# Two reorderings in a convolution, softmax and whitening kernel: when a bias is given out, and when one interpolation is

## Chip, cores and metric

The kernel runs on one core of one Trainium2 chip. The time is the device time of one execution in microseconds, and the median of several runs is given. An engine is named as the profile names it: PE is TensorE, DVE is VectorE, ACT is ScalarE, POOL is GpSimd, SP is SyncE, which here issues most DMAs.

## What is computed

The input x has 4 images of 256 channels and 64x64 pixels, in float32. The first layer is a local attention: a 7x7 convolution with dilation 2 to 128 channels, a 1x1 convolution to 49 channels, a softmax over the 49, and a sum of the 49 shifted copies of x, weighted with the softmax. The second layer whitens the result over groups of 64 channels.

```python
k = lax.conv_general_dilated(x, w1, (1, 1), [(6, 6), (6, 6)], rhs_dilation=(2, 2), ...) + b1
k = lax.conv_general_dilated(k, w2, (1, 1), ...) + b2
attn = jax.nn.softmax(k, axis=1)
shifts = stack([xp[:, :, 2*u:2*u+64, 2*v:2*v+64] for u in range(7) for v in range(7)], axis=1)
x = jnp.einsum('bkchw,bkhw->bchw', shifts, attn)
...
Sigma = EPS * I + einsum('gdm,gem->gde', xc, xc) / m      # groups of 64 channels
for _ in range(5): P = 1.5 * P - 0.5 * (P @ P @ P) @ Sigma_N
X_hat = (P * sqrt(rTr)) @ xc * weight + bias
```

## The kernel before

**The convolution.** The two convolutions have no nonlinearity between them, so the kernel multiplies their weights once and does one 7x7 convolution from 256 to 49 channels. It does it by evaluation and interpolation, in rows and in columns (a Toom-Cook scheme): image rows are combined into 7 row points, each of them is combined along the columns into 7 column points, each point needs a short convolution (six of the row points this way, the seventh directly, line 685), and the outputs are interpolated back, first along the columns and then along the rows. One row point, br, passes through these steps:

- `weights` (line 364) gets the weights of the point. For most points they are loaded from DRAM by a DMA on SP (line 378, `wr<-gd`), which may start once the matmuls of the row point before have left the buffer.
- `row_eval` (line 439) makes the row combination `rb` on DVE, and `col_ops` (line 473) the column points `xh` on DVE, with one copy on ACT (lines 488 and 494). Each `xh` has one buffer, which PE must have left before the next row point is written.
- `conv_bank` (line 520) does the matmuls of a bank of column points into PSUM (lines 538 to 546) and evicts them to `pv` with an ACT copy (line 548). There are three banks a row point, with 3, 3 and 1 column points. Images 1 to 3 use two slots of `pv` in turn, so that row 2 writes over row 0.
- `col_interp` (line 617) interpolates the columns with 20 DVE instructions into `zz`, and a last ACT copy, `end` (line 635).
- After the fifth and the sixth row point, `row_interp` (line 643) interpolates the rows in two parts into `lgx`, the logits. It writes four phases. Each phase gets the convolution's bias in an ACT instruction (line 662).

**The order.** `conv_step(k, i)` (line 738) is given out for each row point k and bank i: the bank's matmuls, then `prepare`, which evaluates bank i for the row point after, and after the last bank the interpolation. The instructions that are given out are then put in order on each engine's queue when the program is built: the planner takes, by its own estimate of when things are ready, the ready instruction that was given out first, except that instructions inside `tc.high_priority()` count as earlier. On the chip each queue then runs in that fixed order.

Two things are put off by hand. The ACT instructions behind an interpolation (`end`) are put on a list `later` and are given out behind the eviction of the second bank of the next row point (lines 552 to 562), each with a dependency that holds it behind that eviction. This holds for the copy of `col_interp` and for the two biases of the first part of `row_interp`, for images 1 to 3. The list is emptied from its end.

**The work beside it.** While the convolution of image b runs, the output of an earlier image is made in eight phases an image, from a plan: `gap(b, j)` (line 1247) gives out `first_half(n)` or `second_half(n)` at eight points between the conv steps. Such a half transposes blocks of x on PE (line 1032) and copies them out of PSUM on ACT (line 1040, `xb`), multiplies them with a banded matrix of the softmax weights (line 1061, `y<-band,xb`), moves the result on ACT (line 1080), transposes it (line 1093), copies it (line 1101, `yt<-tp`, high priority) and adds to the second moments (line 1114). The transposes share three PSUM tiles `tp`. The band is loaded by DMAs on SP (line 994, `band<-sd`) and then transposed in place on DVE (line 1009). `softmax` of an image is in two halves; for image 0 the second half stands in the plan between the conv steps of image 1's rows 0 and 1.

Of the kernel before, what the change touches and what calls it, by code (L numbers as in the profile page):

```python
# [32 lines left out]
def kernel(  # L33
# [55 lines left out]
    def taps(b):  # L89
        return (0,) if b == INF else (0, 1)  # L90

    def pe(ins):
        return tc.keep_in_program_order(ins)
# [203 lines left out]
    @contextmanager  # L297
    def in_order():
        was = strict[0]
        strict[0] = True  # L300
        with tc.high_priority():
            yield
        strict[0] = was
# [198 lines left out]
    def col_eval(src, i):  # L502
        for _ in col_ops(src, i):
            pass
# [10 lines left out]

    slot = {}

    later = []

    def conv_bank(b, br, i, w):  # L520

        if i == 0:
            slot[b, br] = len(slot) % NV if b == 0 else (len(slot) - NV) % 2
        pts = BANKS[i]
        i0 = sum(len(k) for k in BANKS[:i])
        cv = cv_buf[ncv[0] % 2][:, : 3 * PT].rearrange(
            "p (n q b two) -> p n q b two", n=3, two=2, b=Q9
        )
        ncv[0] += 1
        for k, bc in enumerate(pts):  # L530
            terms = [(sr, sc, cc) for sc in taps(bc) for sr in taps(br) for cc in range(NCC)]
            wv = w[bc].rearrange("p c (a r k) -> p c r a k", r=len(taps(br)), a=NCC)
            for j, (sr, sc, cc) in enumerate(terms):

                n = Q9 if j == 0 and bc == INF else Q8
                for h in range(2):
                    pe(
                        nc.tensor.matmul(  # L538
                            cv[h * HB : h * HB + KT, k, sr : sr + n, sc : sc + n],
                            wv[:, sc, sr, cc],  # L540
                            xh[bc][:, :n, h * NCC + cc, :n],
                            start=(j == 0),
                            stop=(j == len(terms) - 1),
                            skip_group_check=True,
                        )
                    )
        with tc.high_priority():
            last = nc.scalar.copy(  # L548
                pv[:K2, slot[b, br], i0 : i0 + len(pts)].rearrange("p n q b -> p (n q b)"),
                cv[:K2, : len(pts)].rearrange("p n q b two -> p (n q b two)"),  # L550
            )
        if i == 1:

            while later:
                tc.add_manual_dep(
                    later.pop()().ins,
                    last.ins.name,
                    mybir.DependencyInfo(
                        mybir.DependencyClass.NoSync, mybir.DependencyReason.DATA
                    ),  # L560
                    reason="later",
                )

    def interpolate(pt, tmp, outs, cut, part=None, pairs=None):

        lo = lambda t: cut(t, 0)
        hi = lambda t: cut(t, 1)
        c0, s1, s2, s3, s4, hh, c6 = (pt[b] for b in (0, 1, 2, 3, 4, 5, 6))
        both = tmp
        if pairs is not None:
            tmp, s1 = tmp[:, 0], tmp[:, 1]
        if part != 1:
            if pairs is not None:  # L580
                add(both, *pairs)
                sub(pairs[1], *pairs)
            else:
                add(tmp, s1, s2)
                sub(s2, s1, s2)
                add(s1, s3, s4)
                sub(s4, s3, s4)
            add(s3, c0, c6)
            madd(s1, tmp, -2.0, s1)
            sub(s3, tmp, s3)  # L590
            madd(tmp, tmp, -30.5, s1)
            sub(s4, s4, s2)
            madd(tmp, s3, 22.5, tmp)
            madd(s1, c0, 1.5, s1)
            madd(tmp, s2, -16.0, tmp)
            madd(s1, c6, -30.0, s1)
            if part is None:
                add(tmp, tmp, s4)
            madd(s3, s1, -1.0 / 6, s3)
            madd(outs[0], lo(s1), 1.0 / 6, hi(c0))  # L600
            if part == 0:
                add(outs[2], lo(c6), hi(s3))
                add(s3, tmp, s4)
        if part != 0:
            madd(hh, tmp if part is None else s3, -1.0 / 9, hh)
            if part is None:
                add(outs[2], lo(c6), hi(s3))
            madd(s4, hh, -3.0, s4)
            sub(s2, s2, hh)
            madd(s2, s4, -1.0 / 15, s2)  # L610
            madd(outs[1], lo(s4), 1.0 / 15, hi(s2))

    def phases(t):

        return [t[..., bass.ds(4 + a - R if a < R else 0, Q8, 4), :] for a in range(4)]

    def col_interp(b, br, part=None):
        at = slot[b, br]
        pt = {
            c: pv[:K2, at, i].rearrange("p q b -> p (q b)").rearrange(  # L620
                "p (q b two) -> p q b two", q=Q9, two=2
            )
            for i, c in enumerate(ORDER)
        }
        outs = phases(zz[:K2, br].rearrange("p q (w two) -> p q w two", two=2))
        cut = lambda t, k: t[:, :, k : k + Q8]
        t = ct.rearrange("p a b -> p (a b)") if b == 0 else spare[:, NTAP:]
        t = t[:K2, : 2 * PT].rearrange("p (n q b two) -> p n q b two", q=Q9, two=2, n=2)
        pair = lambda i: pv[:K2, at, i : i + 4 : 3].rearrange(
            "p n q b -> p n (q b)"  # L630
        ).rearrange("p n (q b two) -> p n q b two", q=Q9, two=2)
        interpolate(pt, t, outs, cut, part, (pair(0), pair(1)))

        def end():
            ins = nc.scalar.copy(outs[3], cut(pt[5], 0))
            return ins

        if part is None and b > 0 and br != ROWS[-2]:
            later.append(end)
        elif part != 0:  # L640
            end()

    def row_interp(b, part):

        pt = {k: zz[:K2, k] for k in range(NP)}
        lg = lgx
        if b == 0:
            lg = store[4].rearrange("p c r w -> p (c r w)")
        lg = lg[:, : SH * W].rearrange("p (r w) -> p r w", w=W)
        outs = phases(lg[:K2])  # L650
        cut = lambda t, k: t[:, k : k + Q8]
        tr = ct.rearrange("p a b -> p (a b)")[:K2, : Q9 * W].rearrange("p (q w) -> p q w", w=W)
        interpolate(pt, tr, outs, cut, part)
        if part == 0:
            done_ = ((0, outs[0]), (2, outs[2]))
        else:
            done_ = ((3, cut(pt[5], 0)), (1, outs[1]))
            logits[b] = lg
        for a, t in done_:

            def end(a=a, t=t):
                return nc.scalar.activation(outs[a], t, AF.Identity, bias=bias[:K2])

            if b > 0 and part == 0:
                later.append(end)
            else:
                end()

# [55 lines left out]
    rows = [(0, br) for br in (1, 2, 3)]  # L724
    NR0 = len(rows)
    rows += [(b, br) for b in range(1, B) for br in ROWS]
    cur, nxt = {}, {}

    def prepare(k, i):

        b, br = rows[k]
        w = weights(b, br, i)
        if i == 0:
            cur["x"] = row_eval(b, br)
        nxt.update(w)
        col_eval(cur["x"], i)

    def conv_step(k, i):
        w = {bc: nxt.pop(bc) for bc in BANKS[i]}
        b, br = rows[k]  # L740
        conv_bank(b, br, i, w)
        end = b > 0 and br == ROWS[-1]
        if end:

            with in_order():
                if i == len(BANKS) - 2:
                    col_interp(b, br, 0)
                elif i == len(BANKS) - 1:
                    col_interp(b, br, 1)
                    row_interp(b, 1)  # L750
        if k + 1 < len(rows):
            prepare(k + 1, i)
        if i == len(BANKS) - 1 and not end:
            last = br == ROWS[-2]
            with in_order() if last else nullcontext():
                col_interp(b, br)
                if last:
                    row_interp(b, 0)
# [17 lines left out]
    def bank(k, i):  # L776
        conv_bank(0, rows[k][1], i, {bc: nxt.pop(bc) for bc in BANKS[i]})
# [60 lines left out]
    direct0(5, 0)  # L838
    col_interp(0, 3)
    row_interp(0, 0)  # L840
    prepare(NR0, 0)
    direct0(5, 1)
# [646 lines left out]
```

## Time and profile before

| | |
|---|---|
| Runs | 747.56 us median (745.64, 747.56, 749.41) |
| The profiled execution | 746.19 us, of which the span of the trace is 744.4 us |
| PE matmul busy | 703.4 us, 94% of the span |
| DVE busy | 611.3 us, 82% |
| ACT busy | 332.5 us, 45% |
| Mean granted PE clock | 0.986 |
| Image 1's convolution on PE, row 0's first matmul to row 5's last | 156.9 to 278.2 us |

In the profile a row of a timeline gives the start and the length in us, the engine, the line, the operation, its output and inputs, and in brackets how long the engine was idle before and what ended that. A table of stages gives for each stretch of time its length, the busy time of PE, PE's weight loads, DVE, ACT and POOL with the number of instructions, then the granted PE clock, the DMA engines' busy share and the GB/s moved.

### The profile page before, as it was taken

How to read it: one execution, taken by the hardware profiler on the slowest of the kernel's cores; microseconds unless marked ns; L12 is line 12 of the kernel's file. 1: busy time of each engine (PE TensorE's matmuls, PEld its weight loads, DVE VectorE, ACT ScalarE, POOL GpSimd, SP SyncE). 2: the span in 40 equal slices, each digit the busy share in tenths (PEclk: the TensorE clock that was granted, in tenths of full speed). 3: DMA queues.
4: the chain of work that ended last, by engine and by line, in shares of the span. 5: the costliest groups of instructions: out<-in, count | busy, mean ns of one | idle time of the engine just before them, and what ended most of it. 6: DMA issues, size and time to landing. Idle time of an engine off the chain costs nothing.

```text
span 744.4 us, 18491 instructions
## 1 busy us (share of the span) xinstructions
PE 703.4 (94%) x7512; PEld 528.3 (71%) x7512; DVE 611.3 (82%) x1268; ACT 332.5 (45%) x953; POOL 51.6 (7%) x52
## 2 busy tenths in 40 slices
PE   6999999997999897999999999999999889998996
PEld 1449543377898794799998958898998678885331
DVE  3789998999999989968995999799969655535575
ACT  1424240255364543466444435735535663322564
POOL 0410070020001110001000100000000000000000
PEclk9999999999899999999999999999999999999999
DMA  8991120147263491076545820534423144371588
GB/s 319 250 319 73 60 88 12 60 147 212 87 193 112 146 317 48 21 245 199 185 128 201 253 69 7 166 108 135 155 64 95 32 149 118 104 296 72 219 357 327
DMA packets 59629, 114.41 MB, mean 154 GB/s; under 512 B 22887, under 2 KB 42008, under 8 KB 58776
## 3 DMA queue, kind: packets, MB, share of 16 engines
q1 hardware_dynamic: 55848, 94.36, 38.7%
q0 software_dynamic: 3696, 18.88, 7.3%
q8 instruction: 59, 0.97, 0.5%
q14 instruction: 26, 0.21, 0.1%
HBM read 65.88 MB, written 47.33 MB: 152 GB/s over the span
## 4 chain that ended last, share of the span: by engine, by line
PE 61%; DVE 28%; ACT 4%; issue 3%; DMA 2%; SPq 0%; DVEq 0%; ACTq 0%
PE cv L538 20%; PE y L1061 12%; PE acc L685 6%; PE tp L1429 4%; PE tp L1093 3%; PE sig L1114 3%; PE cv L685 3%; PE tp L1032 3%; DVE xh L313 3%; DVE pv L313 3%; DVE zz L313 2%; DVE rb L313 2%; PE cv L222 2%; DVE ct L313 2%; DVE band L1009 2%
## 5 line engine op out<-in xcount | busy, mean ns | idle before, releaser
L538 PE MATMUL cv<-xh,wr 128*49 128x128 f32 x4368 | 250.2, 276 | 5.7 <-DVE rm L899 5.3
L538 PEld LDWEIGHTS cv<-xh,wr 128*49 128x49 f32 x4368 | 244.1, 124 | 9.6 <-ACT xh L494 5.5
L1061 PE MATMUL y<-band,xb 128*128 128x224 f32 (+2 forms) x640 | 150.6, 373 | 7.6 <-ACT xb L1040 5.9
L1061 PEld LDWEIGHTS y<-band,xb 128*128 128x128 f32 x640 | 109.1, 192 | 29.0 <-ACT xb L1040 8.9
L548 ACT COPY pv<-cv 113x486 f32<-113x486 f32 (+1 forms) x63 | 30.0, 476 | 86.1 <-PE cv L538 85.8
L1080 ACT ACTIVATE slot<-y,pivot 128x512 f32<-128x512 f32 x53 | 36.6, 738 | 63.5 <-PE y L1061 63.4
L1101 ACT COPY yt<-tp 128x256 f32<-128x256 f32 x128 | 45.6, 378 | 38.8 <-PE tp L1093 37.6
L1032 PE MATMUL tp<-ident,slot 128*128 128x128 f32 x256 | 49.9, 297 | 6.7 <-ACT yt L1101 6.7
L313 DVE SCALAR_TENSOR_TENSOR pv<-pv 113x162 f32<-113x162 f32 x186 | 54.9, 318 | 1.0 <-ACT pv L548 0.4
L1093 PE MATMUL tp<-ident,slot 128*128 128x128 f32 x256 | 52.1, 299 | 3.6 <-ACT yt L1101 1.0
L1009 DVE STREAM_TRANSPOSE band<-band 128x864 f32<-128x864 f32 (+1 forms) x48 | 47.4, 990 | 9.5 <-DMA band<-sd 9.5
L1093 PEld LDWEIGHTS tp<-ident,slot 128*128 128x128 f32 x256 | 41.3, 205 | 13.8 <-issue 4.4
L1032 PEld LDWEIGHTS tp<-ident,slot 128*128 128x128 f32 x256 | 39.9, 205 | 13.0 <-ACT yt L1101 8.0
L941 ACT COPY zt<-d 32x112 f32<-32x112 f32 (+2 forms) x156 | 44.8, 287 | 1.9
L893 ACT ACTIVATE d<-tp,mx 128x49 f32<-128x49 f32 x128 | 37.0, 336 | 17.4 <-DVE mx L888 13.9
L313 DVE SCALAR_TENSOR_TENSOR xh<-ct 128x512 f32<-128x512 f32 x42 | 27.8, 683 | 14.1 <-PE cv L538 13.7
L1114 PE MATMUL sig<-yt 128*64 128x65 f32 x1024 | 36.9, 225 | 0.0
L1114 PEld LDWEIGHTS sig<-yt 128*64 128x64 f32 x1024 | 32.4, 137 | 6.0 <-issue 4.5
L1040 ACT COPY xb<-tp 128x256 f32<-128x256 f32 x87 | 30.5, 376 | 12.9 <-PE tp L1032 12.4
L1040 DVE COPY xb<-tp 128x256 f32<-128x256 f32 x41 | 16.5, 421 | 23.5 <-PE tp L1032 23.5
L685 PE MATMUL acc<-slot,tap 128*49 128x496 f32 (+3 forms) x168 | 34.6, 569 | 0.0
L893 ACT ACTIVATION_READ_ACCUMULATOR d<-tp,mx 128x1 f32 x128 | 30.6, 241 | 0.0
(222 smaller groups left out, 959.2 us busy)
## 6 DMA issues: line engine op xcount, KB each, us to landing
out_dram<-out SPq DMA_DIRECT2D x32, 512.0 KB, 3.4
sd<-zt SPq DMA_DIRECT2D x16, 896.0 KB, 4.2
slot<-in_x_dram POOLq DMA_DIRECT2D x12, 1024.0 KB, 10.0
band<-sd SPq DMA_DIRECT2D x128, 84.0 KB, 2.2
wr<-gd SPq DMA_DIRECT2D x15, 588.0 KB, 3.7
wr<-gd SPq DMA_DIRECT2D x15, 490.0 KB, 3.9
spill<-slot POOLq DMA_DIRECT2D x3, 2048.0 KB, 7.7
back<-spill SPq DMA_DIRECT2D x3, 2048.0 KB, 13.3
```

The lines of the kernel that those rows point to most:

```text
L313: return in_turn(STT(o, a, f, b, ALU.mult, ALU.add))
L538: nc.tensor.matmul(cv[h * HB : h * HB + KT, k, sr : sr + n, sc : sc + n], wv[:, sc, sr, cc], xh[bc][:, :n, h * NCC + cc, :n], start=(j == ...
L685: nc.tensor.matmul(ps[h * HB : h * HB + KT, :, w0:w1_], w[v][:, cc], xs[:, :, cc, w0 + d : w1_ + d], start=(j == 0), stop=(j == len(order) ...
L893: nc.scalar.activation(d[:, h, i], lt[i // NI][:, i % NI, h, :KT], AF.Exp, bias=mx[:, i, h : h + 1], accum_out=s[:, h, i : i + 1],)
L941: ins = nc.scalar.copy(o, i)
L1009: return nc.vector.transpose(f, f)
L1032: nc.tensor.transpose(t[:, cc * P : (cc + 1) * P], xt[:, cc, CR * m : CR * (m + 1), bass.ds(pc, SW, 2)], ident,)
L1040: (nc.vector.tensor_copy if tail else nc.scalar.copy)(xb, t[:, :C])
L1061: nc.tensor.matmul(ps[:, cc, q0 - half * HALF : q1 - half * HALF, :], xb[:, cc * P : (cc + 1) * P], rhs, start=(k == 0), stop=(k == len(PI ...
L1093: nc.tensor.transpose(t[:, cc * P : (cc + 1) * P], yt[:, cc, CR * i : CR * (i + 1), bass.ds(pc, SW, 2)], ident,)
L1101: nc.scalar.copy(yb.rearrange("p a g c -> p (a g) c")[:, :, :GW], t[:, :C].rearrange("p (e c) -> p e c", c=GW),)
L1114: nc.tensor.matmul(sig[g * GW : (g + 1) * GW, cc], yb[:, cc, g, :GW], yb[:, cc, g], start=(count[0] == 0 and cc == 0), stop=(count[0] == 4 ...
```

## The change

The list `later` becomes two lists, one that is emptied behind the second bank's eviction and one behind the third's. The copies of `col_interp` stay on the first. The two biases of the first part of `row_interp` go to the second, for images 1 to 3. And the column interpolation of image 1's row point 0 is no longer given out at the end of its own last conv step, but in the next conv step (row 1's first bank), behind the `prepare` that evaluates the first bank of row point 2. The second half of image 0's softmax is given out between these two places.

```diff
-    later = []
+    later = {1: [], 2: []}
...
-        if i == 1:
-            while later:
+        if i in later:
+            while later[i]:
                 tc.add_manual_dep(
-                    later.pop()().ins,
+                    later[i].pop()().ins,
                     last.ins.name,
...
         if part is None and b > 0 and br != ROWS[-2]:
-            later.append(end)
+            later[1].append(end)
...
             if b > 0 and part == 0:
-                later.append(end)
+                later[2].append(end)
...
-    cur, nxt = {}, {}
+    cur, nxt, waiting = {}, {}, []
...
         if k + 1 < len(rows):
             prepare(k + 1, i)
+        if waiting:
+            col_interp(*waiting.pop())
         if i == len(BANKS) - 1 and not end:
             last = br == ROWS[-2]
+            if (b, br) == (1, 0):
+                waiting.append((b, br))
+                return
             with in_order() if last else nullcontext():
                 col_interp(b, br)
```

## The prediction

> **What bounds the kernel now.** I read the page's busy table first, then the chain that ended last, then PE's timeline for its holes, then a table of stages around each hole, and last the queue of the engine that each hole waits for. The page says which engine matters:
>
> ```profile
> PE 703.4 (94%) x7512; PEld 528.3 (71%) x7512; DVE 611.3 (82%) x1268; ACT 332.5 (45%) x953; POOL 51.6 (7%) x52
> ```
>
> TensorE is the bound, so only its holes are worth something. From 155 us to 600 us its timeline shows just two holes over 1.5 us, one for each half of the change. The table of stages (PE's busy time is the first number after the length, the granted clock the third from the end) shows them:
>
> ```profile
> 182.20:187.60 5.40, 0.09 (x4) 0.04 (x2) 5.40 (x15) 4.98 (x30) 0.00 (x0) 0.75 0.76 238
> 187.60:195.10 7.50, 7.50 (x97) 7.31 (x97) 7.50 (x17) 0.00 (x0) 0.00 (x0) 0.72 0.14 52
> 278.20:291.10 12.90, 9.11 (x68) 7.05 (x66) 11.03 (x25) 5.86 (x14) 0.00 (x0) 0.87 0.28 78
> 429.50:437.80 8.30, 7.89 (x71) 6.36 (x68) 8.23 (x20) 4.51 (x11) 0.00 (x0) 1.00 0.42 121
> 555.00:562.70 7.70, 7.44 (x68) 6.18 (x66) 7.46 (x12) 3.64 (x10) 0.00 (x0) 1.00 0.19 44
> ```
>
> The last three rows are the same work, second_half of one output phase; it takes 7.7 us undisturbed and 12.9 us where the bias stands in the way. Rows one and two are the wait for image 1's third row point and its first bank at the lowered clock: 7.5 us, while the 96 matmuls of row 1's first bank took 5.3 us (170.23 to 175.5).
>
> Who ends the first hole? The timelines of PE, DVE and SyncE:
>
> ```profile
> 183.20 0.68 DVE L309 TENSOR_TENSOR xh<-ct 128x512 f32<-128x512 f32 x1
> 174.66 8.86 SPq L994 DMA_DIRECT2D band<-sd  x12
> 183.62 0.37 SPq L378 DMA_DIRECT2D wr<-gd  x1
> 187.59 7.52 PE L538 MATMUL cv<-xh,wr 128*49 128x128 f32 x96 [5.31 <-DVE rm L899]
> ```
>
> The bracket names the softmax's rm, which no bank reads. The evaluation that the bank does read (xh) ends at 183.88. Its weights (wr) are issued only at 183.62, behind twelve band loads on SyncE. The page gives such a 588 KB load a median of 3.7 us to landing: 187.3, within 0.3 us of PE's start. So the late arrival is a DMA, not the evaluation.
>
> The second hole, ACT, then DVE, then PE:
>
> ```profile
> 277.02 0.56 ACT L548 COPY pv<-cv 113x486 f32<-113x486 f32 x1
> 277.48 0.72 ACT L662 ACTIVATE lgx<-lgx,bias 113x512 f32<-113x512 f32 x1
> 281.65 0.72 ACT L662 ACTIVATE lgx<-lgx,bias 113x512 f32<-113x512 f32 x1 [3.45 <-DVE lgx L306]
> 282.28 0.27 ACT L548 COPY pv<-cv 113x162 f32<-113x162 f32 x1
> 282.46 1.04 ACT L448 COPY rb<-slot 128x1024 f32<-128x1024 f32 x1
> 283.40 0.65 ACT L1101 COPY yt<-tp 128x256 f32<-128x256 f32 x2
> ...
> 279.97 1.08 DVE L1009 STREAM_TRANSPOSE band<-band 128x864 f32<-128x864 f32 x1 [2.66 <-DMA band<-sd]
> 280.97 0.65 DVE L306 TENSOR_TENSOR lgx<-zz 113x512 f32<-113x512 f32 x1
> ...
> 283.83 0.70 PE L1032 MATMUL tp<-ident,slot 128*128 128x128 f32 x2 [3.52 <-ACT yt L1101]
> ```
>
> VectorE waits 2.66 us for a band load, so the second phase of the logits (lgx) is late, so ACT stands before its bias, and behind it stand the third bank's eviction, a row copy and the two yt copies. These yt copies free the transposes' three PSUM tiles, and PE has used all three by 280.3.
>
> **What the Trainium skill says.** "TensorE: Matmul & The Clock Gate", Part 1: The HAM clock gate, says that free-running windows of 3413 ns decide the clock and that an idle window halves it. The trace agrees: clock 0.75 and 0.72 around the first hole, 0.87 over the stage of the second. The same page, under Architectural detail, says that ACT and DVE are strict FIFO; the eviction at 282.28 starts as the waiting bias ends, which agrees. "DMA: Bandwidth & Descriptors", Issuing engines are not separate DMA queues, says that transfers of all issuers share 16 DMA engines; here the band loads of 269.95 to 272.0 landed only at about 279.9, next to two loads of x that POOL issued from 264.72 on. "Perfetto Trace Analysis", Identifying Dependency Chains, says that an instruction waiting for several engines has further waits put in ahead of it; so a bracket with one name, as at 187.59, must be checked, and here I overrule it.
>
> **Part one, the bias.** For each of images 1 to 3 two ACTIVATEs of 0.72 us move from behind the second to behind the third eviction of the last row point. Nothing is added. For image 1 the third eviction is then free at 278.2 (PE ends that bank there) instead of 282.28. What follows it on ACT is decided at compile time by priority and readiness: the row copy L448 (given out earlier, 1.04 us), the bias pair, and the yt copies, which have high priority but need PE's transposes of 278.15 to 278.7. If the copies come ahead of the bias, ACT does eviction 278.2 to 278.5, L448 to about 279.8 (its second half of x lands near 278.7), yt to 280.4, and PE never stops: the stage falls from 12.97 us (278.15 to 291.12) to the 7.77 us of 554.97 to 562.74. That is 5.2 us, 3.5 of them waiting and 1.7 clock. If the later-ready bias goes first, it still waits until 281.65 and the yt copies follow at 282.3: 1.1 us, up to 2.4 if the clock stays up. Image 2's stage has 8.2 us against 7.8, with its bias waiting 1.07 us: between +0.5 (pair ahead of yt) and -0.4. Image 3's pair does not wait (568.07); behind the eviction it costs 0 to 0.7, since three PSUM tiles cover about 1.2 us. I take -5.2 +0.2 +0.5 = -4.5 us, lower bound -5.6, upper bound 0. Does the gain last? The next wait would be the softmax transposes at 310.39, whose last bias ends at 298.8: 11 us of room for 5. PE has no hole over 0.7 us from 291 to 600, so nothing else shows itself as next.
>
> **Part two, the interpolation.** It issues 20 DVE instructions (2 of 113x324, 15 of 113x162, 3 of 113x144), no DMA, and one ACT copy that stays behind row 1's second eviction. At starts 0.41, 0.24 and 0.22 us apart they hold DVE for 0.8 + 3.6 + 0.7 = 5.1 us, between 174.80 and 183.3. Moved behind the third row point's first evaluation and the second half of softmax, the evaluation is ready near 179 instead of 183.88 (row 1's first bank has left xh at 175.5), and the exponentials start near 177.5 instead of 181.1. But wr still lands at about 187.4: SyncE's queue depends on row 1's bank and on band loads, which come from the first softmax, and the interpolation feeds neither. DVE has no idle time there, before or after, so the same work is done by 188. I take 0. Bounds: if SyncE's order changed with it and the hole closed, 5.3 + 2.2 = 7.5 us of PE; of this DVE, which is busy 49.86 of 50 us and 49.79 of 50 us in the stretches 150 to 200 and 200 to 250, lets at most some 5 pass before row 5's last bank (xh ready 276.04, PE there near 276.2). The other bound is the fourth case below.
>
> **Sum.** The profiled execution is 746.19 us: span 744.4 and 1.8 around it; the runs' median is 747.56, 1.4 above. 746.19 - 4.5 = 741.7 for such an execution, 747.56 - 4.5 = 743.1 at the median.
>
> **Rivals.** (1) *The copies pass the bias*: 743.1, its own range 741.0 to 745.0. For it: L448 stood directly behind the third eviction before, so the planner had it ready there, and that lets yt in next. (2) *The bias still leads*: last-in first-out hands out the late phase first, both phases had been ready before the third eviction in the planner's eyes, so ACT waits at 281.65 again. Image 1 gives 1.1, images 2 and 3 take 0.5 back: 747.0, 745.2 to 748.5. (3) *Both holes close*: wr gets ahead of the band loads, 5 us more: 738, 735 to 740; against it, nothing moved feeds SyncE. (4) *Slower: the moved interpolation holds a pv slot.* Row 0 and row 2 of image 1 share slot 0. Row 2's first eviction is at 195.15; the interpolation's last reader, ACT's copy, ends at 186.5. So it decides from a delay of 8.6 us on. If the interpolation falls behind row 2's three evaluations and the band transposes, where the second interpolation now stands (191.8 to 198.9), eviction waits to about 199.2, the xb copies (195.60) behind it on ACT too, and PE's y at 196.04: 4.0 us and one window at half clock, 1.7. With the small gain of (2): 747.56 + 5.7 - 0.6 = 752.7, 749.5 to 756. Against it: it is still given out ahead of row 2's second evaluation.
>
> **How the numbers follow.** A change under 0.5%, 3.7 us, can't be told from none here; the runs before span 745.64 to 749.41. Chances: (1) 0.45, of which 0.29 lies under 743.8; (2) 0.23; (3) 0.09; (4) 0.23, with any other reshuffle of the queues that costs as much, 0.20 above 751.3. Faster 0.29 + 0.09 = 0.38; slower 0.20; same 0.42. The range for 8 in 10 leaves out half of (3) and most of (4): 739 to 751.
>
> **What would show it.** Step one: image 1's second_half near 7.8 us, yt copies ahead of a waiting L662, no PE hole from 280 on. Step two: xh ready near 179 with the hole at 182 still there and ended by a wr load behind twelve band loads. I am wrong on two if PE starts that bank well before 187; on one if L662 waits right behind the third eviction with yt behind it; on the whole if pv evictions wait for DVE near 195.

## The result, and the profile after

| | before | after |
|---|---|---|
| Median | 747.54 us (745.64 to 750.49, 20 runs) | 747.25 us (745.90 to 749.42, 20 runs) |
| Ratio of after to before | | 0.9998, 95% interval 0.9989 to 1.0007 |
| Span of the profiled execution | 744.4 us | 746.3 us |

The interval is 1.3 us wide and includes 1: no change that can be measured. The forecast was 743.1 us. The page of after shows the same bound, TensorE, almost as busy as before:

```profile
PE 706.2 (95%) x7512; PEld 531.1 (71%) x7512; DVE 611.9 (82%) x1268; ACT 331.8 (44%) x953; POOL 50.4 (7%) x52
```

The table of stages of after (columns as above) has the first hole, image 1's second_half, and one stage that had no hole before:

```profile
182.10:188.10 6.00, 0.00 (x0) 0.01 (x1) 6.00 (x16) 2.20 (x7) 0.00 (x0) 0.93 0.76 240
...
279.80:288.00 8.20, 7.59 (x68) 6.32 (x66) 6.42 (x15) 6.53 (x14) 0.00 (x0) 1.00 0.40 118
320.20:330.70 10.50, 7.05 (x19) 4.57 (x20) 5.72 (x17) 4.49 (x13) 0.00 (x0) 0.67 0.57 178
```

The hole at 182 is as long as ever. Image 1's second_half at 280 is closed: 279.83 to 288.04, 8.21 us instead of 12.97. In its place stands a stage at 320 us in which PE works 7 of 10.5 us, at a clock of 0.67.

**The first hole.** SyncE, DVE and PE of after, one timeline each:

```profile
174.54 9.04 SPq L1001 DMA_DIRECT2D band<-sd  x12
183.68 13.18 SPq L378 DMA_DIRECT2D wr<-gd  x4
```
```profile
178.47 0.69 DVE L309 TENSOR_TENSOR xh<-ct 128x512 f32<-128x512 f32 x1
```
```profile
188.12 8.38 PE L539 MATMUL cv<-xh,wr 128*49 128x128 f32 x96 [6.03 <-DMA wr<-gd]
```

The evaluation now ends at 179.16 instead of 183.88, and PE does not start sooner. The weight load is still issued at 183.68, behind the twelve band loads, and here the bracket names it.

**The second hole.** ACT's timeline of after around the moved bias:

```profile
281.37 0.64 ACT L1108 COPY yt<-tp 128x256 f32<-128x256 f32 x2
...
283.82 1.37 ACT L663 ACTIVATE lgx<-lgx,bias 113x512 f32<-113x512 f32 x2
```

The third eviction (279.94), the row copy (280.41) and the yt copies pass ahead, and the bias pair comes behind them, at 283.82. It waits for nothing there.

**The new hole.** PE's timeline of before and of after at the same place, softmax of image 1 and the second_half behind it:

```profile
311.28 10.02 PE L538 MATMUL cv<-xh,wr 128*49 128x128 f32 x176
323.23 0.41 PE L1032 MATMUL tp<-ident,slot 128*128 128x128 f32 x2
...
324.13 3.18 PE L1061 MATMUL y<-band,xb 128*128 128x320 f32 x12 [0.26 <-ACT xb L1040]
327.24 1.15 PE L1114 MATMUL sig<-yt 128*64 128x65 f32 x32
```
```profile
308.20 10.02 PE L539 MATMUL cv<-xh,wr 128*49 128x128 f32 x176
323.14 0.51 PE L1039 MATMUL tp<-ident,slot 128*128 128x128 f32 x2 [2.83 <-ACT yt L1108]
...
324.54 6.13 PE L1068 MATMUL y<-band,xb 128*128 128x320 f32 x12 [0.62 <-ACT xb L1047]
330.60 1.15 PE L1121 MATMUL sig<-yt 128*64 128x65 f32 x32
```

PE comes to row 0's bank 3.08 us earlier than before (308.20 against 311.28) and to its sig matmuls 3.36 us later (330.60 against 327.24). In this profile it loses 6.4 us there: 2.83 waiting for yt, 2.95 because the twelve y matmuls take 6.13 us instead of 3.18 at the lowered clock, and the rest in the shorter waits and slower transposes between.

Who holds the yt copies? ACT's timeline of after, its first yt copies of before, then DVE's timeline of before and of after:

```profile
313.39 0.30 ACT L900 ACTIVATE d<-tp,mx 128x49 f32<-128x49 f32 x1 [5.62 <-DVE mx L895]
...
318.38 3.29 ACT L948 COPY zt<-d 128x56 f32<-128x56 f32 x11
...
322.71 0.65 ACT L1108 COPY yt<-tp 128x256 f32<-128x256 f32 x2
```
```profile
322.06 0.65 ACT L1101 COPY yt<-tp 128x256 f32<-128x256 f32 x2
```
```profile
310.90 1.05 DVE L885 TENSOR_REDUCE mx<-tp 128x8 f32<-128x392 f32 x2 [0.73 <-PE tp L879]
```
```profile
309.38 2.29 DVE L309 TENSOR_TENSOR rb<-rb,rb 128x2048 f32<-128x2048 f32 x1
311.59 1.03 DVE L892 TENSOR_REDUCE mx<-tp 128x8 f32<-128x392 f32 x2
```

On ACT the yt copies stand behind all of the softmax: exponentials, an eviction, the zt copies. These begin when DVE has the maximum, `mx`. PE's transposes of the logits end at 308.2 now, but DVE is in the row combinations of image 2, and the second of these (L309, 2.29 us) is ahead of the maximum in DVE's fixed order. Before, DVE came to the maximum 0.73 us ahead of PE and waited for it, and the first of the yt copies ended at 322.44, 0.79 us before the transposes at 323.23. So an earlier PE could gain some 1.5 us there, and no more. PE came some 3 us earlier as the profile counts time, 4.8 counted from the start of the stage at 280, and DVE did not.

The sum closes. Without its wait PE would have been at the transposes at 320.31 (323.14 less 2.83), 2.92 us earlier than before. DVE reached the maximum at 311.59 instead of 310.17 (310.90 less its wait), 1.42 us later, as in this profile everything stands later from 255 us on (last section). PE gained 4.34 us on DVE; less the 1.52 us of room that leaves 2.82, and the wait is 2.83. For part one alone, below, the same sum gives 3.07, and its wait is 3.07.

### The profile page after: what moved, and what is told of

The parts are those of the page before. It is cut to its first block, busy times and chain, and to the rows that moved or that the text cites. A ratio compares the mean times of both kernels' runs of the same rounds, so it can differ in the third digit from the quotient of the medians.

```text
span 746.3 us, 18490 instructions
## 1 busy us (share of the span) xinstructions
PE 706.2 (95%) x7512; PEld 531.1 (71%) x7512; DVE 611.9 (82%) x1268; ACT 331.8 (44%) x953; POOL 50.4 (7%) x52
## 4 chain that ended last, share of the span: by engine, by line
PE 61%; DVE 24%; ACT 6%; DMA 5%; issue 2%; SPq 1%; DVEq 0%; ACTq 0%
PE cv L539 22%; PE y L1068 13%; PE acc L686 6%; PE tp L1436 4%; PE tp L1100 3%; PE sig L1121 3%; PE tp L1039 3%; DVE zz L313 2%; DMA band<-sd 2%; DVE rb L306 2%; DVE xh L313 2%; DVE pv L313 2%; DVE ct L313 2%; PE cv L686 2%; DVE ct L306 2%
## 5 line engine op out<-in xcount | busy, mean ns | idle before, releaser
L1068 PE MATMUL y<-band,xb 128*128 128x224 f32 (+2 forms) x640 | 154.1, 380 | 7.4 <-ACT xb L1047 5.7
L1068 PEld LDWEIGHTS y<-band,xb 128*128 128x128 f32 x640 | 111.2, 196 | 29.8 <-ACT xb L1047 8.4
```

The costliest lines, as they stand in the source:

```text
L1068: nc.tensor.matmul(ps[:, cc, q0 - half * HALF : q1 - half * HALF, :], xb[:, cc * P : (cc + 1) * P], rhs, start=(k == 0), stop=(k == len(PI ...
```

## Experiments

Theory A: the gain of part one is real, and it is given back near 320 us, where the maximum stands behind image 2's rows on DVE; part two is worth nothing, as the bank at 182 waits for a weight load. Its rivals are named in the expectations. Each kernel was timed beside the kernel before, on several chips; the ratio compares with those runs, whose median was 747.2 to 748.2 us, and is not a quotient of the medians below.

| kernel | median us | ratio, 95% interval |
|---|---|---|
| p1_only | 748.14 | 1.0001, 0.9990 to 1.0012 |
| p2_only | 747.59 | 0.9997, 0.9986 to 1.0009 |
| after_max_first | 743.21 | 0.9944, 0.9928 to 0.9960 |
| before_max_first | 747.42 | 0.9997, 0.9985 to 1.0009 |
| p1_and_max_first | 744.72 | 0.9962, 0.9950 to 0.9975 |
| after_max_first_again | 744.63 | 0.9952, 0.9936 to 0.9968 |
| p1_and_max_first_again | 743.92 | 0.9945, 0.9930 to 0.9959 |
| before_load_early | 755.08 | 1.0101, 1.0082 to 1.0121 |
| after_load_early | 754.34 | 1.0102, 1.0081 to 1.0123 |
| after_load_early_max_first | 756.02 | 1.0111, 1.0096 to 1.0126 |
| before_load_first | 749.28 | 1.0003, 0.9989 to 1.0017 |
| after_load_first_max_first | 749.65 | 1.0023, 1.0012 to 1.0033 |

### Each part alone

Part one alone is the kernel before with the two lists:

```diff
-    later = []
+    later = {1: [], 2: []}
...
-                later.append(end)
+                later[2].append(end)
```

> The bias part alone; every queue but ACT's stands as before. Theory A (the stage at 280 us is won as forecast, and VectorE, which was not made earlier, takes it back at image 2's start because its queue reaches the maxima of image 1's softmax late): second_half at 280 us takes about 8 us instead of 12.9, a new PE hole of 3 to 4 us stands near 320 us behind the yt copies, time 747.2, within 0.3% of before. Theory B (the new hole comes from the moved interpolation): no hole near 320 us, 742.5 to 743.5. Theory C (both holes are chance of the clock windows): hole near 320 under 1 us, time 745 or so.

Part two alone is the kernel before with the interpolation put off:

```diff
+            if (b, br) == (1, 0):
+                waiting.append((b, br))
+                return
```

> The interpolation part alone. Theory A: holes at 182 us (5 to 6 us) and at 280 us (3.5 us) both stay, the bank at 187.6 us still starts when its wr load lands, no hole near 320 us, 747.5. Theory B: holes at 182 and 280 stay and one opens near 320, 750 or more. If the evaluation had been what the bank waited for: the first hole is 4 us shorter, 743 to 745.

PE's timeline of part one alone, then of part two alone:

```profile
283.05 3.18 PE L1061 MATMUL y<-band,xb 128*128 128x320 f32 x12 [0.63 <-ACT xb L1040]
323.28 0.70 PE L1032 MATMUL tp<-ident,slot 128*128 128x128 f32 x2 [3.07 <-ACT yt L1101]
...
324.67 4.23 PE L1061 MATMUL y<-band,xb 128*128 128x320 f32 x12 [0.27 <-ACT xb L1040]
```
```profile
187.64 8.21 PE L538 MATMUL cv<-xh,wr 128*49 128x128 f32 x96 [5.01 <-DVE band L1014]
283.38 0.51 PE L1037 MATMUL tp<-ident,slot 128*128 128x128 f32 x2 [2.97 <-ACT yt L1106]
```

Part one closes the hole at 280 and opens the one at 323; part two does neither and leaves the hole at 182. Neither moves the median. In part one's profile the stage at 280 is 4.6 us shorter, and from the transposes behind row 0's bank to the sig matmuls behind the new hole PE takes 4.8 us longer: 1.05 of that is in the twelve y matmuls at the lowered clock, against 2.95 in the profile of after. The new hole belongs to part one alone, so it is not a by-product of the moved interpolation.

### The maximum ahead of the row combination

If the maximum's place in DVE's queue is what takes the gain back, putting it first must bring the gain out, and must do nothing in the kernel before, where it waits for PE. The edit holds image 2's `sub(r[0], r[0], r[1])` (the row combination for row 2) behind the negated maximum of image 1's first softmax half. It only orders instructions on one engine.

```diff
-            sub(r[0], r[0], r[1])
+            behind_max(b, sub(r[0], r[0], r[1]))
...
-        nc.vector.tensor_scalar(mx, mx, -1.0, None, ALU.mult)
+        neg = nc.vector.tensor_scalar(mx, mx, -1.0, None, ALU.mult)
+        if b == 1:
+            maxima[b, pc] = neg
```

> Both parts, and the 2.29 us row combination of image 2's row point 2 held behind the maxima of image 1's softmax on VectorE. Theory A: the maxima are about 2.2 us earlier, the hole near 320 us shrinks from 2.8 to under 1 us, y behind it runs at full clock (3.2 us instead of 6.1), 742 to 743.5. Theories B and C: the hole does not follow the maxima, 746.5 to 747.5.

> The kernel before with the same hold on the row combination alone. Theory A: the maxima wait for PE there already (0.73 us idle), no hole near 320 us to close: 747.5, no change. If VectorE's order were worth something by itself: 745 or less.

DVE and PE of the changed kernel with this edit:

```profile
306.63 1.03 DVE L903 TENSOR_REDUCE mx<-tp 128x8 f32<-128x392 f32 x2
...
307.78 2.28 DVE L309 TENSOR_TENSOR rb<-rb,rb 128x2048 f32<-128x2048 f32 x1
```
```profile
319.37 3.18 PE L1081 MATMUL y<-band,xb 128*128 128x320 f32 x12 [0.62 <-ACT xb L1060]
```

Of the hole near 320 a wait of 0.62 us is left, the twelve y matmuls run at full clock, and the time falls to 743.2 us. That is 0.56% below before (0.40 to 0.72), the size forecast for part one. In the kernel before the same edit makes DVE wait for PE, and the time stays:

```profile
313.29 1.05 DVE L896 TENSOR_REDUCE mx<-tp 128x8 f32<-128x392 f32 x2 [3.09 <-PE tp L890]
```

Both halves together show the cause: the edit is worth nothing alone, part one is worth nothing alone, and the two are worth 3 to 4 us, with part two (here) or without it (next).

### Is part two worth anything in that version?

This kernel has the two lists and the maximum first, but not the put-off interpolation. It was run twice, the second time beside the full version on one chip.

> Part one of the change and the maximum put first, without part two: the interpolation of image 1's row 0 stays where it was before. Theory A (part two is worth nothing, because the bank at 182 us waits for its weight load): 743.2 us within 1, as with both parts; the hole at 182 is 5.0 to 5.5 us and is ended near 187.5, the hole at 280 is closed, none is over 1 us near 320. Theory B (part two gives room on VectorE which the later stages use): 745 us or more, and a hole over 1 us either at 280 or near 320.

> The same program as the changed kernel with the maximum first, measured again beside the next one on one chip. Theory A (part two is worth nothing): the two agree within 1 us, both 743 to 745 us. Theory B (part two is worth the 1.5 us by which the first two measurements differed): this one is 1 to 2 us ahead of the next one again.

> The same program as part one with the maximum first, without part two. Theory A: within 1 us of the run above, 743 to 745 us; no stage from 182 to 330 us is longer than there but by the granted clock. Theory B: 1 to 2 us above it, and the profile shows a stage in which PE waits longer than there.

The first time, on another chip, it was 1.5 us behind the full version, more than Theory A allowed; the second time 0.7 us ahead of it. The four intervals overlap. So no worth of part two is shown, and a difference of about 1 us isn't excluded by the times. The profiles show why so little comes of it. In the kernel before PE has a hole of 1.32 us that ends at 232.59. With part two this hole is 1.04 us or less, without it 1.32 to 2.25, but PE leaves the place at about the same time: at 232.25 to 232.68 us in the four profiles with part two, at 232.28 to 233.13 in the five without.

### The weight load out of the queue

If the bank at 182 waits for a load that is ready but stands behind twelve band loads, the load should be issued elsewhere. First on POOL:

```diff
-            nc.sync.dma_start(wt, gd[br][:, s0 : s0 + ns])
+            queue = nc.gpsimd if (b, br, i) == (1, 2, 0) else nc.sync
+            queue.dma_start(wt, gd[br][:, s0 : s0 + ns])
```

> The kernel before with one edit: the first weight load of image 1's row 2 is issued by POOL and no longer by SP, where it stands behind twelve band loads. Theory A (the hole at 182 us is the queue in front of that load): the load is issued near 175.6 us, lands near 179.5, and the bank starts when its evaluation is ready, near 184 us; the hole is 1.5 to 2.2 us instead of 5.3. Of the 3.6 us or, with the clock, up to 5.8, some part lasts: 742.0 to 746.5 us; nothing lasts (747.5) if VectorE, which has almost no idle time from 150 to 250 us, is what sets the start of the later banks. Theory B (the evaluation or the softmax is what the bank waits for): hole of 5 us, 747.5 us.

> The changed kernel with the same edit of the weight load. Here the evaluation is ready near 179 us, before PE ends the bank ahead at 182.3. Theory A: the bank follows within 0.7 us and the hole at 182 is gone, which is the first place where part two shows a worth: 1.5 to 2.2 us more of PE time at 184 than the kernel before with this edit. As the wait behind the rows of image 2 near 320 us is still there, the time is 743 to 747.5 us. Theory B (part two is worth nothing even then): the hole is as long as in the kernel before with this edit.

> The changed kernel with the early weight load and with the maximum of image 1's first softmax half ahead of the row combination of image 2. Theory A: no hole over 1.5 us at 182, 280 or 320 us; if what is won at 182 lasts, 738 to 741.5 us; if VectorE takes it back by 280 us, 743 us within 1.5. Theory B: no better than 743.2 us, with a hole of 5 us still at 182.

All three became slower by 7.5 to 8.3 us (1.0% to 1.1% of 747.22 us), which no theory had. PE's timeline of the kernel before with this edit shows what was won and what was lost; the page's part on DMA issues has the load:

```profile
184.69 7.17 PE L539 MATMUL cv<-xh,wr 128*49 128x128 f32 x96 [2.77 <-DMA wr<-gd]
...
252.27 5.52 PE L1062 MATMUL y<-band,xb 128*128 128x320 f32 x12 [5.96 <-ACT xb L1041]
...
288.28 3.35 PE L539 MATMUL cv<-xh,wr 128*49 128x128 f32 x32 [8.90 <-DVE xh L313]
```
```profile
wr<-gd POOLq DMA_DIRECT2D x1, 588.0 KB, 8.5
```

The load was issued at 176.06, 7.6 us earlier, and PE started only 2.9 us earlier, because the load took 8.5 us to land instead of some 3.9 (183.62 to about 187.5). In the changed kernel with this edit the hole is 2.74 us, although the evaluation is ready at 179: Theory A had expected it gone. So even with the early load part two is worth nothing; it is the transfer itself that PE waits for. (In the kernel before, SyncE did not issue all through the 8.9 us of the twelve band loads: for 2.6 us, up to 181.80, it waited for an earlier band load to land.)

The loss comes later. At the place where before has its hole of 232.59, PE is still 4.7 us ahead of it. But the planner, presumably because it now takes that bank to be early, gave DVE another order from 204 us on (some 90 of its 1,268 instructions stand elsewhere, and a few on ACT and SP), and PE waits 6 us near 250 and 9 us near 288. To see whether POOL had a part in it, the load was left on SP and put in front of the band loads (the hint that keeps SP's later loads in place is left out of the diff):

```diff
-            nc.sync.dma_start(wt, gd[br][:, s0 : s0 + ns])
+            with tc.high_priority() if (b, br, i) == (1, 2, 0) else nullcontext():
+                wload[b, br, i] = nc.sync.dma_start(wt, gd[br][:, s0 : s0 + ns])
```

> The kernel before, with the first weight load of image 1's row 2 still on SP, but in front of the twelve band loads instead of behind them. Theory A (the hole at 182 us is the queue in front of the load): it is issued near 176 us, and the bank starts at 184 to 185 us, when its evaluation is ready or the load has landed, with a hole of 1.7 to 2.8 us instead of 5.3. In total it is slower than before, 750 to 757 us, because the same shift of VectorE's order as with the load on POOL comes with it: a stall of VectorE over 4 us on a band load between 235 and 255 us and PE holes of 5 us or more near 250 and 288 us. Theory B (it was POOL that made those runs slow): 742 to 747 us.

> The changed kernel with the maximum first and with that load in front of the band loads. The evaluation is ready near 179 us here. If the load lands by 182.3 us, PE does not stop there (hole under 1 us), which would be the first worth of part two; if it lands near 184.6 us, as the load on POOL did, the hole is 2 to 3 us with or without part two. In total 749 to 757 us where VectorE's order is shifted as with the load on POOL, 739 to 743 us where it is not.

PE and DVE of the kernel before with this edit:

```profile
185.14 8.37 PE L541 MATMUL cv<-xh,wr 128*49 128x128 f32 x96 [3.20 <-ACT d L905]
...
281.55 3.66 PE L541 MATMUL cv<-xh,wr 128*49 128x128 f32 x32 [8.11 <-DVE xh L313]
```
```profile
276.20 1.08 DVE L1021 STREAM_TRANSPOSE band<-band 128x864 f32<-128x864 f32 x1 [1.26 <-DMA band<-sd]
...
280.71 0.69 DVE L313 SCALAR_TENSOR_TENSOR xh<-xh,rb 128x512 f32<-128x512 f32 x1
```

It was issued at 176.23 and PE started at 185.14, 2.45 us earlier than before. The version with part two started at 184.55, with a hole of 2.54 us. With part two the evaluation is ready near 179, so it isn't what the bank waits for; the landing of this load is not in the traces, and that it ends the wait is read from PE's start. The times are 1.0003 and 1.0023 of before: the first is neither of the two forecasts (750 to 757, 742 to 747), the second as expected for a shifted order. The loss is smaller than with POOL and of the same kind. The evaluation of row 5's last bank ends at 281.40 instead of 276.04, as the order of DVE now has a waiting band transpose and both lgx ahead of it. PE, which finishes the bank before it at 273.4, waits 8.11 us. DVE's stall of over 4 us on a band load, which the run with POOL had (6.55 us at 243.56), did not come here (1.26 us), which may be why the loss is smaller.

What this leaves open: what the bank at 182 would be worth with VectorE's order kept as it was. No such kernel was tried, so that the changed order is the cause of the loss is argued from these rows and not shown by an experiment.

## Why the prediction was wrong, step by step

**PE is the bound, and its holes are at 182 and 280: right.** After the hole at 280 is closed and no new one of that size is opened (after_max_first) the time falls by about 4 us, a little less than the 5.0 us by which the stage is shorter in its profile.

**Part two is worth 0: right.** The evaluation came at 179.16 (forecast: near 179), and the hole stayed, ended by the load behind twelve band loads. The reason given, that the load is late because it stands in SyncE's queue, was half of it. Without the queue the load takes more than twice as long: it then shares the DMA engines with the band loads and an x load. Between 172 and 180 us their share is 0.99 in the kernel before and 1.02 with the load in front. Of the 5.3 us an earlier issue took away 2.5 to 2.9.

**Part one brings 5.2 us at the stage itself, less 0.2 and 0.5 at images 2 and 3: right in mechanism, sizes close.** The copies passed the bias, as in case 1. The stage fell from 12.97 to 8.21 us, 4.76 instead of 5.2. Image 2's stage went from 8.22 to 8.47 us (0.25 lost, near the 0.2 set aside), image 3's stayed at 7.77 (0.5 had been set aside).

**"Does the gain last? The next wait would be the softmax transposes at 310.39, whose last bias ends at 298.8: 11 us of room for 5.": this is the step that failed.** The room was read from PE's own data, the logits. They were ready, and PE did run its transposes at 307.15, 3.1 us earlier than before. The reader of those transposes was not asked. It is DVE, in fixed order and full, and its row of the kernel before (310.90, waiting 0.73 us for PE) gives its room: 0.73 us. From there a chain on ACT leads back to PE: before, the first yt copy ended 0.79 us ahead of the transposes (323.23) that need its tile. That makes 1.5 us of room where the prediction had 11. The rest of the gain came out as a wait at 320, 2.83 us, and the lowered clock behind that wait (2.95 us in after, 1.05 in part one alone) took what was left. "PE has no hole over 0.7 us from 291 to 600, so nothing else shows itself as next" is true of the trace and proves nothing: a wait that an engine would meet if it came earlier has no hole in the trace of the slower kernel. What shows it is how little the other engines wait or lead there: 0.73 us of DVE and 0.79 of ACT.

**The rivals.** Case 4, a held pv slot, did not occur. Case 2's number, 747.0, is near the result, but its mechanism, a bias that still leads, did not occur either. The case that came true, part one works and the wait moves on by 40 us, had no number among the rivals. That the result lies inside the range of 739 to 751, and that no measurable change had the highest chance, 0.42, is luck: neither was reckoned from this case.

**The version that beats both** is the change with the maximum first: 743.21 and 744.63 us in two measurements, 0.56% and 0.48% below before. Between 190 and 670 us its profile has no PE hole over 1.3 us.

## What to carry to other kernels

Before a closed hole is counted as a gain, follow the bound engine to each later point where another engine reads its result and hands something back, and read that engine's place in its queue, not the readiness of the data. The idle time of the other engine ahead of its reading instruction, and the time by which what it hands back is early, are the room there; a gain beyond them needs that engine's order changed too. And an edit that makes one thing earlier also changes what an automatic planner does with everything behind it: compare the order on each engine before crediting or blaming the edit itself.

## What the runs showed of the hardware

The cost of a short hole in clock can differ from one profile to the next with nothing changed ahead of it. Near 250 us PE has two short holes, of about 0.8 and 1.2 us, and twelve equal matmuls behind them, in all nine profiles in which the weight load was not moved. These took 3.18 us in the profiles of before, p2_only and twice after_max_first, and 4.87 us in those of after, p1_only, before_max_first and twice p1_and_max_first. The rows of before and of p1_only:

```profile
251.67 3.18 PE L1061 MATMUL y<-band,xb 128*128 128x320 f32 x12 [1.24 <-ACT xb L1040]
```
```profile
251.37 4.87 PE L1061 MATMUL y<-band,xb 128*128 128x320 f32 x12 [1.23 <-ACT xb L1040]
```

From 251.6 to 255.0 us the granted clock was 1.00 in the first and 0.52 in the second. In p1_only no instruction ahead of that place had been moved. The Trainium skill, "TensorE: Matmul & The Clock Gate", Part 1: The HAM clock gate, says that the clock is halved after an idle window of about 3.4 us, and that these windows run freely and are not reset when a kernel starts. Here holes of 0.8 and 1.2 us were enough in five of nine profiles, so the measurement differs from the first. It fits the second: before and after begin these matmuls at 251.67 and 251.64 us of their own time, and only after loses the clock. Where the windows lay is not in the traces. A difference of 1.7 us between two profiles can therefore have nothing to do with the edit, which is one more reason to go by the medians.

A load's time to landing is no constant. The same 588 KB took about 3.9 us behind the band loads, beside two smaller weight loads (issued at 183.62; the landing is read from PE's start), and 8.5 us when it was issued among the band loads. The busy share of the DMA engines was high in both: 0.89 from 183.6 to 187.5 us in the first, 1.01 from 176.0 to 184.5 in the second. That fits the Trainium skill, "DMA: Bandwidth & Descriptors", Issuing engines are not separate DMA queues: whichever engine issues, transfers run on the same 16 DMA engines. The bank started 8.6 to 8.8 us after the load's early issue by POOL, and 8.2 to 8.9 us after its early issue by SP.
